# One transform of length 136 for whole graphs in place of two of length 80, in a two-layer graph network

## The chip, the cores and the metric

The kernel runs on one core of one Trainium2 chip. A core has five engines with an instruction queue each: TensorE (PE: matrix multiplies; its weight loads are listed apart as PEld), VectorE (DVE), ScalarE (ACT), GpSimd (POOL) and SyncE (SP). In this kernel SP only issues DMAs, and ACT issues some beside its own work; all DMAs run on the same 16 DMA engines. The metric is the device time of one execution in microseconds (us). Everything is float32. In the profile one float32 multiply is two MATMUL records, so counts of records are twice those of the matmul calls in the code.

## The reference, cut to what matters

128 graphs of 128 nodes with 256 features go through two layers, each with a layer norm, a relu and a residual around it. The change concerns the convolution path of layer 0:

```python
h = relu(layernorm(x))                      # 128 graphs x 128 nodes x 256
h1 = relu(bn1(conv1(h)))                    # conv1: width 1, 256 -> 256
h2 = bn2(conv2(h1))                         # conv2: 17 taps along the nodes, padding 8, 256 -> 256
x_conv = relu(h2 + h)
A = exp(-dist(h @ w_se.T)) * adj            # the edges
x_nmp = A @ relu(h @ w_msg.T)               # the messages
out = GRU([x_conv, x_nmp], h)               # the gates r, z, n
```

conv2 is computed through a Fourier transform along the nodes: transform the taps once, transform the graphs, multiply each frequency by a 256x256 matrix, transform back.

## The kernel before, in words

Blocks of four graphs (`BB`), 32 of them. conv2 takes windows of 64 outputs (`OUTW`) with a transform of length `LW` = 80, so a graph is two windows; 80 rows of a transform are 40 pairs (`NP_`), real and imaginary part. The program runs in five stages.

1. **Heads, first half** (blocks 0 to 15, function `heads`). Per block: layer norm (`head_stats`, `head_norm` on DVE, one POOL power), transpose to features on partitions and relu (`head_turn`, L212 and L213, which also stores the result to DRAM, `htd`), conv1 (`head_conv1`, L226 to L230), and the transform of its output (`head_spectra`, L241), whose results are copied from PSUM into `X`, a tile in SBUF with all frequencies of 64 graphs (`HG`), by DVE (L247) and ACT (L249). In between, `some_spectra` makes the taps' transforms (`weight_spectra`, L165): 8 units of 64 output channels (`WCH`), each 64 matmul calls on 17 of 128 partitions, four at once on four groups of 32 partitions, copied to `sp` (two buffers, L171 and L173) and stored by one DMA per unit to `vd` in DRAM (L175).
2. **Frequencies, first half** (`spectral`). For each pair, six matmul calls of 256 columns (three real products, L312 and L317; pair 0 has four calls, L302), with a sum of the weights on POOL (L309), a combination of `X` on DVE (L307), a copy on ACT (L314) and the final add on DVE (L318). The weights `v` come from `vd` by SP (L294, three buffers of two pairs), the results `ys` go to `yd` in DRAM four pairs at a time (L321).
3. **Heads, second half**, blocks 16 to 31, into the same `X`. The weights of the gates are loaded here.
4. **Frequencies, second half**, with sums of the gates' weights on POOL between the pairs (`gate_weights`).
5. **Gates.** Per block: messages (L516), the inverse transform (`conv_out`: for each half of the channels four calls of 128 columns on `ym`, L498, and one of 256 columns on `yr`, L501, into one PSUM bank; then one DVE and one ACT instruction, L504 and L505), edges (L536, L548, L551 to L553), the messages' sums (L563), the GRU's products (L612) and layer 1 (L877, L937 and others) turn by turn. `beside_gates` is a generator that says in which turn each part of the next block stands; what it doesn't use of the turns goes to layer 1. `load(i)` fetches a block's `ht`, `at`, `ym`, `yr` on SP.

In the first stage the order on all engines is the order written in the program. From then on POOL, and until the last stage of frequencies SP too, keep the written order; the others are placed by the scheduler of the language. PSUM has eight banks, taken in turn (`bank`).

Of the kernel before, what the change touches and what calls it, by code (L numbers as in the profile page):

```python
# [13 lines left out]
P = 128  # L14
EPS = 1e-5
KW = 17
PAD = 8
BB = 4
HG = 64
OUTW = 64  # L20
LW = 80
NP_ = LW // 2
WCH = 64
NR = 2 * LW - P
# [50 lines left out]
def gnn_kernel(ctx: ExitStack, tc: tile.TileContext, io, out0: bass.AP, out1: bass.AP):  # L75
# [6 lines left out]

    NBH = HG // BB
    NH = B // HG

    cst = ctx.enter_context(tc.tile_pool(name="cst", bufs=1))
    front = ExitStack()
    hc = front.enter_context(tc.tile_pool(name="hc", bufs=1))
# [13 lines left out]
    fd = hc.tile([P, 2 * LW], F32)  # L102
# [46 lines left out]
    vd = dram.tile([C, D // WCH, P, LW, WCH], F32, tag="vd", name="vd")  # L149
    yd = [dram.tile([HG, 2, LW, D], F32, tag=f"yd{h}", name=f"yd{h}") for h in range(NH)]  # L150

# [6 lines left out]
    def weight_spectra(pool, c, q, w2):  # L158

        sp = pool.tile([P, LW, WCH], F32, tag="sp", name="sp", bufs=2)  # L160
        for t in range(WCH // 16):
            ps = [bank() for _ in range(4)]
            for j in range(4):
                for r in range(4):
                    nc.tensor.matmul(ps[r][:, j * LW:(j + 1) * LW], w2[32 * r:32 * r + KW, 4 * t + j, :],  # L165
                                     gt[32 * r:32 * r + KW, :], start=True, stop=True)
            for r in range(4):
                o0 = t * 16 + 4 * r
                dst, s = sp[:, :, o0:o0 + 4], ps[r][:, :4 * LW].rearrange("p (j d) -> p d j", j=4)
                if r == 3 and t < WCH // 16 - 1:  # L170
                    nc.vector.tensor_copy(dst, s)  # L171
                else:
                    nc.scalar.copy(dst, s)  # L173
            yield
        nc.scalar.dma_start(vd[c, q], sp)  # L175
# [56 lines left out]

    def head_spectra(X, i):
        h1 = h1s.pop(i)
        g0 = (i * BB) % HG
        for c in range(C):
            xv = X[:, c].rearrange("p a k (w g) -> p (a k) w g", w=2)
            for h in range(BB // 2):
                ps = bank()
                for bb in range(2):  # L240
                    nc.tensor.matmul(ps[:, bb * 2 * LW:(bb + 1) * 2 * LW], h1[:, 2 * h + bb, c * P:(c + 1) * P], fd,  # L241
                                     start=True, stop=True)
                s = ps[:, :4 * LW].rearrange("p (g w d) -> p d w g", g=2, w=2)
                dst = xv[:, :, :, g0 + 2 * h:g0 + 2 * h + 2]
                for w in range(2):
                    if h:
                        nc.vector.tensor_copy(dst[:, :, w], s[:, :, w])  # L247
                    else:
                        nc.scalar.copy(dst[:, :, w], s[:, :, w])  # L249

    def heads_begin(wk, xk, ahead, h):

        i = h * NBH
        for k in range(ahead):
            head_load(xk, ahead, i + k, nc.scalar)
        yield
        for k in range(3):
            head_stats(wk, i + k)
            yield
            if k < 2:  # L260
                head_norm(i + k)
        head_turn(wk, i)

    def heads(wk, xk, ahead, X, h, between):

        i0, i1 = h * NBH, (h + 1) * NBH
        for i in range(i0, i1 + 1):
            if i + ahead < i1:
                head_load(xk, ahead, i + ahead, nc.sync)
            if i < i1:  # L270
                head_conv1(wk, i)
            between()
            if i + 1 < i1:
                head_turn(wk, i + 1)
            if i + 2 < i1:
                head_norm(i + 2)
            between()
            if i > i0:
                head_spectra(X, i - 1)
            if h == 0 and i % 2:  # L280
                between()
            if i + 3 < i1:
                head_stats(wk, i + 3, h1s[i] if h else None)

    def spectral(bp, X, h, amid):

        for p0 in range(0, NP_, 4):
            amid.get(p0, lambda: None)()
            ys = bp.tile([P, 4, 2, D], F32, tag="ys", name="ys", bufs=2)
            for p in range(p0, p0 + 4):  # L290
                if p % 2 == 0:
                    v = bp.tile([P, C, D // WCH, 4, WCH], F32, tag="v", name="v", bufs=3)
                    for c in range(C):
                        nc.sync.dma_start(v[:, c], vd[c, :, :, 2 * p:2 * p + 4, :].rearrange("q i d o -> i q d o"))  # L294
                vr, vi = v[:, :, :, 2 * (p % 2), :], v[:, :, :, 2 * (p % 2) + 1, :]
                a, d = X[:, :, p, 0, :], X[:, :, p, 1, :]
                y = ys[:, p - p0]
                ps = bank()
                if p == 0:
                    for k, (u, w) in enumerate(((a, vr), (d, vi))):  # L300
                        for c in range(C):
                            nc.tensor.matmul(ps[:, k * D:(k + 1) * D], u[:, c], w[:, c], start=c == 0, stop=c == C - 1)  # L302
                    nc.scalar.copy(y.rearrange("p k o -> p (k o)"), ps)
                    continue
# [3 lines left out]
                vs = bp.tile([P, C, D // WCH, WCH], F32, tag="vs", name="vs", bufs=3)  # L308
# [11 lines left out]
            for w in range(2):  # L320
                nc.scalar.dma_start(yd[h][:, w, 2 * p0:2 * p0 + 8, :].rearrange("g d o -> g (d o)"),  # L321
                                    ys[w * HG:(w + 1) * HG].rearrange("p a k o -> p (a k o)"))

# [7 lines left out]
    def gate_weights():  # L331
        tt = nc.gpsimd.tensor_tensor
        for k in range(3):
# [9 lines left out]
    with front as es:  # L343
        hk = es.enter_context(tc.tile_pool(name="hk", bufs=1))
        xp = es.enter_context(tc.tile_pool(name="xp", bufs=1))
        X = xp.tile([P, C, NP_, 2, P], F32)
        order = es.enter_context(ExitStack())
        order.enter_context(tc.manual_schedule(engines={nc.gpsimd.engine}))
        sync_order = order.enter_context(ExitStack())
        sync_order.enter_context(tc.manual_schedule(engines={nc.sync.engine}))  # L350
        with ExitStack() as ws:

            ws.enter_context(tc.manual_schedule())

# [5 lines left out]
            taps = [taps_load(wp, *todo[0], nc.sync, split=4)]  # L360
# [3 lines left out]
            def some_spectra(k=1):  # L364
                for _ in range(k):
                    if not spectra and todo:
                        spectra.append(weight_spectra(wp, *todo.pop(0), taps.pop(0)))
                    if spectra and next(spectra[0], STOP) is STOP:
                        spectra.pop(0)
                        if len(todo) > 1:  # L370
                            taps.append(taps_load(wp, *todo[1], nc.scalar))
                        some_spectra()
# [16 lines left out]
            some_spectra()  # L389
            next(consts)  # L390
            head_norm(1)
            head_stats(hk, 2)
            some_spectra()
            heads(hk, xk, ahead, X, 0, some_spectra)
# [3 lines left out]
        xk = es.enter_context(tc.tile_pool(name="xk1", bufs=1, reuse_waits="tile"))  # L398
        bp = es.enter_context(tc.tile_pool(name="bp", bufs=1, reuse_waits="tile"))
# [5 lines left out]
        sw = [gw.tile([P, 3, 3, P], F32, name=f"sw{k}") for k in range(3)]  # L405
# [6 lines left out]
        begin = heads_begin(hk, xk, 3, 1)  # L412
        sums = gate_weights()
        amid = {p: lambda: next(begin, None) for p in range(16, NP_, 4) if p != 20}
        spectral(bp, X, 0, amid)
        for _ in begin:
            pass

        def gate_loads():
            yield  # L420
            small_loads()
            yield
            yield
            nc.sync.dma_start(wih[:, :C], io["wih"][:D].rearrange("(c p) o -> p c o", p=P))
            yield
            yield
            nc.sync.dma_start(wih[:, C:], io["wih"][D:].rearrange("(c p) o -> p c o", p=P))
            yield
            yield
            nc.sync.dma_start(whh, io["whh"].rearrange("(c p) o -> p c o", p=P))  # L430

        loads = gate_loads()
        heads(hk, xk, 3, X, 1, lambda: next(loads, None))
        sync_order.close()
        spectral(bp, X, 1, {p: lambda: next(sums, None) for p in range(4, NP_, 4)})
# [3 lines left out]

    wk = ctx.enter_context(tc.tile_pool(name="wk", bufs=1, reuse_waits="tile"))  # L440
# [5 lines left out]
    def load(i):  # L446
        h, g0 = divmod(i * BB, HG)
# [6 lines left out]
        y = yd[h].rearrange("g w d o -> g (w d) o")[g0:g0 + BB]  # L454
        nc.sync.dma_start(ym, y[:, :P, :].rearrange("g r o -> r g o"))
        for b in range(BB):
            nc.sync.dma_start(yr[b * NR:(b + 1) * NR, :], y[b, P:, :])
# [3 lines left out]
    idr = wk.tile([P, BB, N - OUTW], F32)  # L461
# [28 lines left out]
    def conv_out(i):  # L490
# [3 lines left out]
        xc = wk.tile([P, C, T], F32, tag="xc", name="xc", bufs=2)  # L494
        for o in range(C):
            ps = bank()
# [671 lines left out]
```

## Time and profile before

Three runs took 1923.13, 1923.68 and 1927.98 us. The profiled execution took 1919.48 us, its span from the first to the last instruction 1917.7 us.

| stage | us from the span's start | length | PE busy | DVE | ACT | POOL | DMA share | GB/s |
|---|---|---|---|---|---|---|---|---|
| heads, blocks 0 to 15, and the taps | 0 to 173 | 173.0 | 160.3 | 113.2 | 87.7 | 22.0 | 0.81 | 298 |
| frequencies, first 64 graphs | 173 to 280 | 107.0 | 106.0 | 55.8 | 16.3 | 49.6 | 0.84 | 276 |
| heads, blocks 16 to 31 | 280 to 386 | 106.0 | 104.2 | 79.0 | 48.9 | 18.9 | 0.52 | 190 |
| frequencies, last 64 graphs | 386 to 489.5 | 103.5 | 102.7 | 49.1 | 15.0 | 57.7 | 0.83 | 279 |
| gates and layer 1 | 489.5 to 1917.7 | 1428.2 | 1417.1 | 1006.8 | 552.5 | 460.9 | 0.36 and 0.34 | 95 |

A busy PE in the profile is one with a matmul in flight, not one at its peak: matmuls overlap in the pipeline, so what an instruction costs is read from the distance between the starts of two groups, not from the mean time of one. The DMA share is the part of the time for which the 16 engines carried packets; packets that overlap can push it over 1.

### The profile page before, as it was taken

What the parts mean: (1) busy time and instruction counts of PE and PEld (TensorE: products, weight loads), DVE (VectorE), ACT (ScalarE), POOL (GpSimd) and SP (SyncE); (2) the same over time, 40 slices, a digit from 0 to 9 for tenths busy, and PEclk for the clock granted to TensorE, in tenths of its full rate; (3) what the DMA queues carried; (4) which work ended last, traced back from release to release, by engine and by line L of the source; (5) the groups of instructions that cost most, each with busy time, mean ns of one, the idle gap of its engine ahead of it and who ended that gap; (6) DMA issues with size and microseconds to landing.
All of it is one profiled execution on the core that took longest, in us unless ns stands there. A gap on an engine that the chain in (4) does not pass through costs nothing.

```text
span 1917.7 us, 30432 instructions
## 1 busy us (share of the span) xinstructions
PE 1890.3 (99%) x10610; PEld 1646.4 (86%) x10610; DVE 1303.9 (68%) x3247; ACT 720.5 (38%) x1555; POOL 609.1 (32%) x678
## 2 busy tenths in 40 slices
PE   8999999999999999999999999999999999999998
PEld 7888889988788888888888888888888888888887
DVE  5676557744677777777666677777756677787643
ACT  4553114411333343343343443333343434334334
POOL 1012531255234334433322233433322233443300
PEclk9999999999999999999999999999999999999999
DMA  8786896379842333333234433233334434222135
GB/s 322 288 312 226 297 311 235 121 241 306 256 117 73 74 95 76 81 90 106 71 94 97 130 97 87 73 82 108 75 90 97 144 72 107 65 78 71 36 92 151
DMA packets 248872, 265.81 MB, mean 139 GB/s; under 512 B 106866, under 2 KB 223943, under 8 KB 244239
## 3 DMA queue, kind: packets, MB, share of 16 engines
q1 hardware_dynamic: 236639, 196.70, 36.9%
q10 hardware_dynamic: 12080, 67.16, 9.0%
q8 instruction: 85, 1.39, 0.3%
q14 instruction: 68, 0.56, 0.1%
HBM read 178.66 MB, written 85.14 MB: 138 GB/s over the span
## 4 chain that ended last, share of the span: by engine, by line
PE 88%; DMA 4%; DVE 4%; issue 2%; ACT 1%; POOL 1%; SPq 0%; ACTq 0%; POOLq 0%; DVEq 0%
PE bank L612 45%; PE bank L317 6%; PE bank L516 5%; PE bank L937 5%; PE bank L877 5%; PE bank L226 4%; PE bank L312 3%; PE bank L563 3%; PE bank L498 3%; PE bank L241 3%; PE bank L165 2%; PE bank L501 1%; PE bank L788 1%; PE bank L856 1%; DMA v<-vd 1%
## 5 line engine op out<-in xcount | busy, mean ns | idle before, releaser
L612 PE MATMUL bank<-t,sw 128*128 128x256 f32 x1152 | 291.6, 380 | 0.7 <-DVE u L504 0.7
L625 POOL TENSOR_TENSOR u<-u,m 128x256 f32<-128x256 f32 x128 | 93.2, 728 | 612.7 <-ACT m L623 545.0
L612 PEld LDWEIGHTS bank<-t,sw 128*128 128x128 f32 x1152 | 215.8, 191 | 31.1 <-issue 2.3
L612 PE MATMUL bank<-t,wih 128*128 128x256 f32 x768 | 197.2, 379 | 0.0
L612 PEld LDWEIGHTS bank<-t,wih 128*128 128x128 f32 x768 | 143.4, 190 | 19.3 <-issue 0.5
L309 POOL TENSOR_TENSOR vs<-v 128x512 f32<-128x512 f32 x78 | 101.3, 1318 | 114.8 <-DMA v<-vd 49.4
L516 PE MATMUL bank<-wms,ht 128*128 128x259 f32 x512 | 124.1, 385 | 0.0
L226 PE MATMUL bank<-wc,ht 128*128 128x256 f32 x512 | 121.4, 391 | 1.6 <-ACT ht L213 1.6
L612 PE MATMUL bank<-xn,wih 128*128 128x256 f32 x384 | 114.9, 381 | 3.6 <-DVE xn L566 3.6
L612 PE MATMUL bank<-t,whh 128*128 128x256 f32 x384 | 115.0, 381 | 0.0
L612 PE MATMUL bank<-xc,wih 128*128 128x256 f32 x384 | 114.8, 381 | 0.0
L937 PE MATMUL bank<-w,hh 128*125 128x256 f32 (+9 forms) x480 | 113.5, 380 | 1.0 <-DVE hh L882 1.0
L226 PEld LDWEIGHTS bank<-wc,ht 128*128 128x128 f32 x512 | 98.0, 196 | 16.7 <-ACT ht L213 3.5
L516 PEld LDWEIGHTS bank<-wms,ht 128*128 128x128 f32 x512 | 98.3, 192 | 15.1
L612 PE MATMUL bank<-ht,whh 128*128 128x256 f32 x384 | 109.9, 380 | 0.0
L877 PE MATMUL bank<-ax,w 128*128 128x500 f32 (+8 forms) x416 | 107.0, 396 | 0.7 <-DMA w<-in_w_dram 0.7
L520 ACT ACTIVATE msg<-msg 128x512 f32<-128x512 f32 x64 | 40.3, 630 | 174.1 <-DVE msg L517 174.1
L630 DVE TENSOR_TENSOR u<-bank,u 128x256 f32<-128x256 f32 x128 | 53.7, 420 | 73.6 <-PE bank L612 73.5
L196 POOL TENSOR_TENSOR rs<-ve,mhalf 128x4 f32<-128x4 f32 x32 | 32.3, 1009 | 217.8 <-DVE ve L194 217.8
L307 DVE SCALAR_TENSOR_TENSOR s<-X 128x256 f32<-128x256 f32 x78 | 47.3, 612 | 79.4 <-PE bank L317 79.1
L937 PEld LDWEIGHTS bank<-w,hh 128*125 128x125 f32 (+9 forms) x480 | 84.3, 177 | 19.2 <-DVE hh L882 1.4
L657 ACT ACTIVATE nn<-nn,vec 128x512 f32<-128x512 f32 x64 | 46.2, 722 | 133.4 <-DVE nn L656 133.4
(187 smaller groups left out, 4279.5 us busy)
## 6 DMA issues: line engine op xcount, KB each, us to landing
v<-vd SPq DMA_DIRECT2D x80, 512.0 KB
vd<-sp ACTq DMA_DIRECT2D x8, 2560.0 KB
yd<-ys ACTq DMA_DIRECT2D x40, 512.0 KB
w<-in_w_dram SPq DMA_DIRECT2D x40, 512.0 KB
htd<-ht ACTq DMA_DIRECT2D x32, 512.0 KB
ht<-htd SPq DMA_DIRECT2D x32, 512.0 KB
ym<-yd SPq DMA_DIRECT2D x32, 512.0 KB
xt<-in_xT_dram SPq DMA_DIRECT2D x32, 512.0 KB
```

What stands on the lines that cost most here:

```text
L226: nc.tensor.matmul(pv[:, bb, :], ht[:, c, b * N:(b + 1) * N], wc1[:, c, :], start=c == 0, stop=c == C - 1)
L241: nc.tensor.matmul(ps[:, bb * 2 * LW:(bb + 1) * 2 * LW], h1[:, 2 * h + bb, c * P:(c + 1) * P], fd, start=True, stop=True)
L309: nc.gpsimd.tensor_tensor(vs, vr, vi, op=ALU.add)
L312: nc.tensor.matmul(p1[:, :D], a[:, c], vs[:, c], start=c == 0, stop=c == C - 1)
L317: nc.tensor.matmul(ps[:, k * D:(k + 1) * D], u[:, c], w[:, c], start=c == 0, stop=c == C - 1)
L498: nc.tensor.matmul(ps[:, b * N:(b + 1) * N], ym[:, b, o * P:(o + 1) * P], idm, start=b == 0, stop=False)
L516: nc.tensor.matmul(ps[:, :D + 3], ht[:, c, b * N:(b + 1) * N], wms[:, c, :], start=c == 0, stop=c == C - 1)
L563: nc.tensor.matmul(ps[:, b * N:(b + 1) * N], msg[:, b, c * P:(c + 1) * P], e[:, b, :], start=True, stop=True)
L612: nc.tensor.matmul(ps, w, d, start=n == 0, stop=n == len(pairs) - 1)
L625: nc.gpsimd.tensor_tensor(got["u4"], got["u2"], got["m5"], op=ALU.add)
L877: nc.tensor.matmul(pv[:, q - q0, :], w1s[k5 + g][:, c, q * P:(q + 1) * P], xv[:, c], start=c == 0, stop=c == C - 1)
L937: nc.tensor.matmul(ps[:n1, :D], hh[:, q, at:at + n1], w2s[k5 + g][:, q, :], start=q == 0, stop=q == HID // P - 1)
```

## The change

The transform has length 136, which holds a whole graph with its padding (128 + 16 would be 144; 136 is enough because what wraps around falls on the padding's zeros). `X` then holds 68 pairs for all 128 graphs, so there is one stage of heads for all 32 blocks and one of frequencies. `X` takes 139 KB of a partition, so the taps are transformed in 32 units of 16 output channels instead of 8 of 64, two half units per block of heads, over nearly the whole stage. `vd` has a new layout, [c, pairs of pairs, partition, unit, 4, 16]: a load of `v` reads 4 KB in one piece per partition (1 KB pieces before), and the store of a unit writes pieces of 256 bytes (20 KB before). `ys` is stored pair by pair, 2 KB pieces (8 KB before). In `conv_out`, 128 of the 136 rows are `ym` and the other 8 are `yr`, multiplied on four groups of 32 partitions; four PSUM banks are held at once, eight DVE instructions take the place of two, and all of it stands in one turn. `edges` stands four turns later relative to the messages. The sums of the gates' weights for one of the three matrices are made after the stage of frequencies, in a tile opened there; `X` is now the first tile on its side of the memory, with the tiles of the gates stage over it.

```diff
-HG = 64
-OUTW = 64
-LW = 80
+LW = 136
-WCH = 64
-NR = 2 * LW - P
+WCH = 16
+NR = LW - P
...
-    vd = dram.tile([C, D // WCH, P, LW, WCH], F32, tag="vd", name="vd")
-    yd = [dram.tile([HG, 2, LW, D], F32, tag=f"yd{h}", name=f"yd{h}") for h in range(NH)]
+    vd = dram.tile([C, NP_ // 2, P, D // WCH, 4, WCH], F32, tag="vd", name="vd")
+    yd = dram.tile([B, LW, D], F32, tag="yd", name="yd")
...
-        for t in range(WCH // 16):
+        n = WCH // 4
+        for j0 in range(0, n, 2):
+            jn = 2
             ps = [bank() for _ in range(4)]
-            for j in range(4):
+            for j in range(jn):
                 for r in range(4):
-                    nc.tensor.matmul(ps[r][:, j * LW:(j + 1) * LW], w2[32 * r:32 * r + KW, 4 * t + j, :],
+                    nc.tensor.matmul(ps[r][:, j * LW:(j + 1) * LW], w2[32 * r:32 * r + KW, j0 + j, :],
...
-        nc.scalar.dma_start(vd[c, q], sp)
+        nc.scalar.dma_start(vd[c, :, :, q].rearrange("u i d o -> i u (d o)"), sp.rearrange("p (u d) o -> p u (d o)", d=4))
...
                 for bb in range(2):
-                    nc.tensor.matmul(ps[:, bb * 2 * LW:(bb + 1) * 2 * LW], h1[:, 2 * h + bb, c * P:(c + 1) * P], fd,
+                    nc.tensor.matmul(ps[:, bb * LW:(bb + 1) * LW], h1[:, 2 * h + bb, c * P:(c + 1) * P], fd,
...
-                for w in range(2):
-                    if h:
-                        nc.vector.tensor_copy(dst[:, :, w], s[:, :, w])
-                    else:
-                        nc.scalar.copy(dst[:, :, w], s[:, :, w])
+                if h:
+                    nc.vector.tensor_copy(dst, src)
+                else:
+                    nc.scalar.copy(dst, src)
...
-                    v = bp.tile([P, C, D // WCH, 4, WCH], F32, tag="v", name="v", bufs=3)
-                    for c in range(C):
-                        nc.sync.dma_start(v[:, c], vd[c, :, :, 2 * p:2 * p + 4, :].rearrange("q i d o -> i q d o"))
+                v = bp.tile([P, C, D // WCH, 4, WCH], F32, tag="v", name="v", bufs=3)
+                for c in range(C):
+                    nc.sync.dma_start(v[:, c], vd[c, p // 2])
...
-            for w in range(2):
-                nc.scalar.dma_start(yd[h][:, w, 2 * p0:2 * p0 + 8, :].rearrange("g d o -> g (d o)"),
-                                    ys[w * HG:(w + 1) * HG].rearrange("p a k o -> p (a k o)"))
+            nc.scalar.dma_start(yd[:, 2 * p:2 * p + 2, :], y)
...
-        for o in range(C):
-            ps = bank()
+        pg = [bank()[:, :C * N].rearrange("p (o n) -> p o n", o=C) for _ in range(BB)]
+        for b in range(BB):
+            for o in range(C):
+                nc.tensor.matmul(pg[b][:, o, :], ym[:, b, o * P:(o + 1) * P], idm, start=o == 0, stop=False)
+
+        for o in range(C):
             for b in range(BB):
-                nc.tensor.matmul(ps[:, b * N:(b + 1) * N], ym[:, b, o * P:(o + 1) * P], idm,
-                                 start=b == 0, stop=False)
-
-            nc.tensor.matmul(ps.rearrange("p (b n) -> p b n", b=BB)[:, :, OUTW:], yr[:, o * P:(o + 1) * P], idr,
-                             start=False, stop=True)
-            u = wk.tile([P, T], F32, tag="el", name="u", bufs=2)
-            nc.vector.scalar_tensor_tensor(u, ps, sc2[:, o:o + 1], ht[:, o, :], op0=ALU.mult, op1=ALU.add)
-            nc.scalar.activation(xc[:, o, :], u, AF.Relu, bias=sh2[:, o:o + 1])
-            yield
+                g = slice(32 * b, 32 * b + NR)
+                nc.tensor.matmul(pg[b][:, o, :], yr[g, o * P:(o + 1) * P], idr[g, :], start=False, stop=o == C - 1)
+        for b in range(BB):
+            g = slice(b * N, (b + 1) * N)
+            for o in range(C):
+                nc.vector.scalar_tensor_tensor(xc[:, o, g], pg[b][:, o, :], sc2[:, o:o + 1], ht[:, o, g],
+                                               op0=ALU.mult, op1=ALU.add)
+        for o in range(C):
+            nc.scalar.activation(xc[:, o, :], xc[:, o, :], AF.Relu, bias=sh2[:, o:o + 1])
+        yield
...
             for _ in inverse:
                 yield
+            next(ends, None)
+            yield
+            yield
+            yield
+
             edges(i)
-            yield
-            next(ends, None)
             yield
             yield
             yield from x_nmp(i)
```

## The prediction

> **What bounds the kernel now.** I read the page first, for the busy share of the engines and the DMAs slice by slice, and then the stages (the table above).
>
> ```profile
> PE 1890.3 (99%) x10610; PEld 1646.4 (86%) x10610; DVE 1303.9 (68%) x3247; ACT 720.5 (38%) x1555; POOL 609.1 (32%) x678
> DMA  8786896379842333333234433233334434222135
> ```
>
> PE is the bound almost everywhere: 27 us of idle in the span, so time is won by fewer or narrower matmuls and lost where PE waits. The DMA row names the danger: in the first 13 slices, the stages that change, the DMAs are busy at 0.5 to 0.9. Next, PE's groups, for counts:
>
> ```profile
> L317 PE MATMUL bank<-v,s 128*128 128x256 f32 x312 | 80.6, 381 | 1.0 <-issue 0.8 <-DVE s L307 0.2
> L312 PE MATMUL bank<-vs,X 128*128 128x256 f32 x312 | 80.5, 379 | 0.8 <-POOL vs L309 0.8
> L241 PE MATMUL bank<-fd,h 128*128 128x160 f32 x512 | 78.1, 307 | 2.3 <-ACT X L249 2.3
> L165 PE MATMUL bank<-gt,w 17*128 17x80 f32 x1024 | 42.9, 301 | 7.7 <-DMA gt<-in_gt_dram 3.9 <-DMA w<-in_w2t_dram 2.4 <-DVE X L247 0.7
> ```
>
> Costs are read from starts in PE's timeline. A block of heads without taps:
>
> ```profile
> 305.37 3.62 PE L226 MATMUL bank<-wc,ht 128*128 128x256 f32 x16
> 308.82 1.04 PE L212 MATMUL bank<-ident,ln 128*128 128x128 f32 x8
> 309.69 2.34 PE L241 MATMUL bank<-fd,h 128*128 128x160 f32 x16
> 311.87 1.46 PE L226 MATMUL bank<-wc,ht 128*128 128x256 f32 x6
> ```
>
> It costs 3.45 + 0.87 + 2.18 = 6.50 us: 0.216 per record of 256 columns, 0.136 of 160, 0.109 of 128; 136 columns come to 0.116 on this line. With taps between:
>
> ```profile
> 114.77 3.62 PE L226 MATMUL bank<-wc,ht 128*128 128x256 f32 x16
> 118.32 1.13 PE L165 MATMUL bank<-gt,w 17*128 17x80 f32 x32
> 119.38 1.09 PE L212 MATMUL bank<-ident,ln 128*128 128x128 f32 x8
> 120.40 1.18 PE L165 MATMUL bank<-gt,w 17*128 17x80 f32 x32
> 121.52 2.44 PE L241 MATMUL bank<-fd,h 128*128 128x160 f32 x16
> ```
>
> From 114.77 to 121.52 is 6.75 us, less 3.45 and 0.87 leaves 1.215 us per group of 32 such records. A smaller group on four row groups is that of the edges:
>
> ```profile
> 1147.60 0.59 PE L612 MATMUL bank<-t,whh 128*128 128x256 f32 x2
> 1148.13 0.50 PE L548 MATMUL bank<-lt 5*128 5x128 f32 x8
> 1148.56 0.70 PE L612 MATMUL bank<-ht,sw 128*128 128x256 f32 x2
> 1149.10 0.59 PE L612 MATMUL bank<-t,sw 128*128 128x256 f32 x2
> ```
>
> 1.50 us for it and two pairs of 0.43: 0.63 us for 8 records. The line through 8 and 32 gives 0.83 us for 16, of which 0.43 doesn't depend on the number. Last, DMAs that write pieces of 412 bytes to DRAM (block outputs, 703 to 705 us):
>
> ```profile
> GB/s 338 321 338 321 321 321 330 272 280 247 214 231 140 115 99 132 124 99 131 99 82 90 178 96 161 112 72 120 128 112 104 128 176 96 144 88 24 80 16 136
> DMA packets 831, 0.33 MB, mean 165 GB/s; under 512 B 831, under 2 KB 831, under 8 KB 831
> ```
>
> They start at 330 GB/s (338/16 engines: 19.5 ns per piece) and fall to about 110 within 0.7 us of this window.
>
> **What the Trainium skill says.** *TensorEngine Tiling (Array Packing)*, Key Properties: a change of tiling mode drains TensorE; the 0.43 us per group agrees. *DMA: Bandwidth & Descriptors*, Why small descriptors are slow: a fixed 3 cycles per packet, 11 instead of 8 for 256 bytes; with its 435 GB/s over 16 engines that is an estimate of 13 ns per piece. The same page, Specifications: under 512 bytes the engine does a read-modify-write; the fall to 110 GB/s fits that, but those pieces also begin and end at odd addresses, and the new ones are aligned 256 bytes, which no row of before shows. Its section Issuing engines are not separate DMA queues: ACT's and SP's transfers share the 16 engines, so `vd` stores delay the loads of `x` too.
>
> **The change part by part**, in span time.
>
> *Frequencies.* Before: 952 records (L317 624, L312 312, L302 16) x 0.216 = 205.6 us, in 210.5. After: 67 pairs x 12 + 8 = 812, 175.4 us: 30.2 less. One start of a stage instead of two, and the 1 us of block 16's transposes is elsewhere: I allow 3 us of stalls instead of 4.9. 178.5, so -32. DMAs: per pair 0.79 MB in 2.6 us as before, loads in 4 KB pieces instead of 1 KB, stores in 2 KB. POOL's sum (1318 ns) reads runs of 16 elements instead of 64; up to 2.6 us per pair it stays hidden behind PE, and I take it unchanged, as its count of elements is. DVE (0.61 + 0.68 us) and ACT (0.37 and one DMA issue) have room too.
>
> *Heads, PE.* Per block 3.45 + 0.87 + 16 x 0.116 = 6.18 instead of 6.50; two half units of 0.83 each: 7.83 us. Together 32 x 6.18 + 64 x 0.83 = 251 us against 32 x 6.50 + 32 x 1.215 = 247. So on PE alone nothing is won. In the first stage of before 10.2 us passed per block (the chain has L241 at 102.0, 112.6, 121.6 and 132.7) with 6.5 + 2.5 x 1.215 = 9.5 of work: 0.7 of waiting.
>
> *Heads, the others per block.* ACT: 7 tap copies (355 ns for 320 elements, about 0.33 for 272), 2 of `ht` at 0.55, 2 of `h` at 0.63, 2 of `X` at 0.33, three DMA issues at 0.33 to 0.45: 6.5 us. DVE: 8 statistics (2.3), 4 norms (1.4), 2 adds (1.4), two copies of `X` and one of taps (1.2): 6.3. DMA: 1.31 MB of `x`, `ht` and taps at the 369 GB/s of the best window of the first stage, 3.55 us, and 4352 pieces of 256 bytes, 272 per engine. At 13 ns: 3.5; at 19.5, the flowing price of a larger piece: 5.3; I take 15: 4.1. Sum 7.65 us (7.1 to 8.85). Three resources thus stand at 6.5 to 7.8 us, and `sp` has two buffers: unit n+2 may be copied only when the store of unit n has landed, about one block after its issue. Behind that ACT copy stand the next `ht`, `h` and `X` copies, for which PE's banks wait. I take PE's 7.83 and the 0.7 of waiting: 8.5. The stage: 18 us until block 0 (20 before, a smaller first load of taps), 30 x 8.5, two blocks without taps at 6.4, the last transform 1.9: 288 us against 173 + 106 = 279. +9.
>
> *Heads to frequencies.* The tiles of the frequency stage lie over those of the heads: in the order of the built program the first load of `v` waits for one of the last L241. Two loads of 512 KB and their latency: PE idle 4.5 us. Before, they were issued from 148.6 us on, 24 us ahead of the stage. +4.5.
>
> *Frequencies to gates.* Before, `ht`, `at` and `ym` of block 0 were loaded while frequencies ran:
>
> ```profile
> 477.57 0.52 SPq L452 DMA_DIRECT2D ht<-htd  x1
> ...
> 494.85 0.34 SPq L452 DMA_DIRECT2D ht<-htd  x1
> ```
>
> with L317 until 489.5; only block 1's load waited for `X`. Now block 0's waits too, behind it all of SP's queue, and `ym` for the last `yd` store. PE is idle some 3.5 us; part of it is taken from the 3.6 us that L612 waits for `xn` at 505. +3.
>
> *Gates.* `conv_out`: 16 K=8 records in one row-tiled group 0.83 instead of 4 x 0.216 = 0.86: nothing. DVE: 8 x about 0.25 instead of 2 x 0.75, 0.5 us more per block, hidden as DVE is busy 77% there; uncovered it would be 16 us in all. The later edges keep a matmul order without a wait that the trace shows. The third weight sum, 4.3 us on POOL, precedes gates that need POOL only later. 0.
>
> Sum: -32 + 9 + 4.5 + 3 = -15.5. The profiled execution (1919.5) would become 1904; the median of the runs is 4.2 above it: **1908 us**.
>
> **Rivals.**
> *The stores make the DMAs the bound of the heads*, without a penalty for writes: at 19.5 ns or with ACT held at issuing (issues behind full queues took up to 2.0 us, 37 us into the span), a block takes 9.0 to 9.7 us, the stage 303 to 324: 1923 to 1944. For it: DMA share 0.81 already in the first stage. Against: the average needed, 78 MB in 288 us = 271 GB/s, is below the 298 there. It decides from 8.8 us per block, so against the likeliest case the sign turns at about 18.5 to 19.5 ns per piece.
> *Narrow writes back up* as the 412-byte ones did: 30 ns per piece (double) gives 8.2 + 3.55 = 11.7 us per block, +105 us, 2010; the 110 GB/s give 10.1 + 3.55, +165 us, 2075 or more. For it: the fence above. Against: alignment, and the stores of 4000-byte pieces, whose ends are odd too, run at 404 GB/s (1089.5 to 1090.5 us).
> *The heads stay at PE's 7.83*, for the two half units are evened out over the stage: 20 us better, 1888.
> *That the change does less than it says* can't be: the matmuls are counted in the program.
>
> **How the numbers follow.** Likeliest 0.47 (its own range 1895 to 1917), stage at PE 0.10, DMA-bound 0.24, narrow writes 0.19. About 0.3% is what a measurement of this kernel can tell: faster means under 1917.9, slower over 1929.5. Faster 0.56 (the first two, less 0.01), same 0.10 (0.09 of it from the DMA-bound case, whose low end is there), slower 0.34. The range runs from 1885 to 2015: it holds the first three cases and the mild half of the fourth.
>
> **What would show it.** L317 and L312 near 268 records each per line and product, frequencies in 176 to 181 us; a heads stage with blocks of 8.5 us and L241 groups of 1.86. DMA share in the heads under 0.9 says the stores flow; near 1, with ACT `sp` waiting for `vd<-sp` and PE for ACT, is the second case, and packets at under 200 GB/s the third. Wrong otherwise: POOL at more than 2.6 us per pair, or L612 waiting for DVE in the gates.

## The result, and the profile after

The changed kernel takes 2145.45 us (median of 4 runs, 2142.83 to 2148.35) against 1923.41 us before (4 runs): a ratio of 1.1163, 95% interval 1.1139 to 1.1187. The forecast was 1908 us with a range up to 2015; it missed on the slow side. The spans of the profiled executions are 2142.6 and 1917.7 us, 224.9 us apart, and that difference is accounted for below.

The page of the changed kernel, its engines and the rows of TensorE's granted clock and of the DMAs in 40 slices:

```profile
PE 1959.1 (91%) x10854; PEld 1682.7 (79%) x10854; DVE 1297.4 (61%) x3361; ACT 739.6 (35%) x1586; POOL 585.1 (27%) x667
PEclk8878877789999999999999999999999999999999
DMA  7555565559997423323243333423423342331225
```

TensorE idles 183 us instead of 27. In the first nine slices, the heads, its clock is at 0.7 to 0.8 and the DMAs are at 0.5 to 0.7: nothing is full there, and yet the stage is slow. The stages, read from TensorE's timeline as before:

| stage | before, us | after, us | difference | forecast |
|---|---|---|---|---|
| heads | 173.0 + 106.0 | 481.0 | +202.0 | +9 |
| idle between heads and frequencies | in the stages | 4.0 | +4.0 | +4.5 |
| frequencies | 107.0 + 103.5 | 180.2 | -30.3 | -32 |
| idle between frequencies and gates | in the stages | 4.7 | +4.7 | +3 |
| gates and layer 1 | 1428.2 | 1472.8 | +44.6 | 0 |

The groups of TensorE that answer to those shown of before (columns: records | busy us, mean ns | idle before them and what ended it):

```profile
L298 PE MATMUL bank<-v,s 128*128 128x256 f32 x268 | 68.8, 379 | 0.0
L293 PE MATMUL bank<-vs,X 128*128 128x256 f32 x268 | 69.9, 384 | 1.1 <-POOL vs L290 1.1
L241 PE MATMUL bank<-fd,h 128*128 128x136 f32 x512 | 114.4, 410 | 0.0
L165 PE MATMUL bank<-gt,w 17*128 17x136 f32 x1024 | 87.2, 366 | 122.2 <-ACT sp L173 118.1 <-DMA w<-in_w2t_dram 4.1
```

The frequencies have the 268 records a line and product that were forecast. In the heads the durations differ: L241 takes a mean of 410 ns for 136 columns, where 160 columns took 307 before, and L165 waits 118 us for ScalarE's copies of `sp`. What ScalarE does meanwhile is in its own timeline of one block, its transfer issues (ACTq) and the copies behind them, with idle time and what ended it in brackets:

```profile
207.23 0.38 ACTq L175 DMA_DIRECT2D vd<-sp  x1
207.65 4.89 ACTq L153 DMA_DIRECT2D w<-in_w2t_dram  x1
212.64 1.25 ACT L173 COPY sp<-bank 128x272 f32<-128x272 f32 x4 [4.78 <-issue]
...
214.91 0.33 ACTq L214 DMA_DIRECT2D htd<-ht  x1
...
222.29 0.38 ACTq L175 DMA_DIRECT2D vd<-sp  x1
222.71 4.14 ACTq L153 DMA_DIRECT2D w<-in_w2t_dram  x1
```

The store of 4352 pieces (L175) itself is issued in 0.38 us. The next issue on ScalarE, the taps load of L153, takes 4.89 us, and the copies stand behind it. From one block's first L226 to the next it is now 14.9 us in the median (14.0 to 17.1) instead of the 8.5 forecast. TensorE in the same block:

```profile
208.09 0.50 PE L165 MATMUL bank<-gt,w 17*128 17x136 f32 x4
213.07 1.56 PE L165 MATMUL bank<-gt,w 17*128 17x136 f32 x12 [4.49 <-ACT sp L173]
214.56 3.50 PE L241 MATMUL bank<-fd,h 128*128 128x136 f32 x16
217.90 3.62 PE L226 MATMUL bank<-wc,ht 128*128 128x256 f32 x16
```

After the wait, L241's 16 records take 3.34 us from start to start; the forecast had 1.86. The windows of two microseconds over it (columns: busy us of PE, PEld, DVE, ACT and POOL, then the granted clock, the DMA share and GB/s) say why:

```profile
207.00:209.00 2.00, 1.59 (x19) 1.15 (x12) 1.48 (x5) 0.63 (x1) 0.00 (x0) 1.00 0.40 89
209.00:211.00 2.00, 0.00 (x0) 0.00 (x0) 0.00 (x0) 0.00 (x0) 0.00 (x0) 0.90 0.99 221
211.00:213.00 2.00, 0.00 (x0) 0.00 (x0) 0.00 (x0) 0.36 (x2) 0.00 (x0) 0.50 0.86 186
213.00:215.00 2.00, 1.93 (x14) 1.68 (x15) 0.27 (x1) 1.88 (x6) 0.00 (x0) 0.50 1.17 354
215.00:217.00 2.00, 2.00 (x11) 2.00 (x11) 0.39 (x2) 1.26 (x4) 0.00 (x0) 0.50 0.92 368
217.00:219.00 2.00, 2.00 (x13) 1.87 (x13) 1.08 (x4) 0.39 (x1) 0.00 (x0) 0.89 0.01 2
```

The clock falls to 0.50 during the wait and stays there for some 4 us of the work behind it. All compute engines stand still from 209 to 211 us, while the DMAs run, and at 217 to 219 the DMAs stand still: store and work overlap only in part.

In the gates the loss has one name. TensorE's waits from 670 us on (us in total, times, longest), and the place in one block:

```profile
PE bank L753 <- ACT hn L749: 36.0, 28, 2.3
PE bank L481 <- DMA ht<-htd: 4.7, 1, 4.7
PE bank L577 <- DVE xc L467: 3.2, 1, 3.2
```

```profile
1307.69 0.38 PE L740 MATMUL bank<-ident,xl 128*100 128x128 f32 x2
1307.91 1.03 PE L577 MATMUL bank<-ht,whh 128*128 128x256 f32 x4
1310.17 0.98 PE L753 MATMUL bank<-ae,hn 100*128 100x212 f32 x4 [1.23 <-ACT hn L749]
```

Between the transposes of L740 and the matmul of L753, which needs their normalised result, lies one turn of gate matmuls. The kernel before has no wait at this matmul, its L788:

```profile
L788 PE MATMUL bank<-ae,hn 100*128 100x212 f32 x128 | 29.0, 349 | 0.0
```

There it was three turns: the second `yield` of `conv_out` and the turn of the edges lay between the two. In the changed kernel `conv_out` has only one `yield`, and `next(ends)` stands ahead of the edges and of the turns put before them.

### The profile page after: what moved, and what is told of

Its sections match the earlier page's. It is cut to its first block, busy times and chain, and to the rows that moved or that the text cites. A ratio compares the mean times of both kernels' runs of the same rounds, so it can differ in the third digit from the quotient of the medians.

```text
span 2142.6 us, 31052 instructions
## 1 busy us (share of the span) xinstructions
PE 1959.1 (91%) x10854; PEld 1682.7 (79%) x10854; DVE 1297.4 (61%) x3361; ACT 739.6 (35%) x1586; POOL 585.1 (27%) x667
## 4 chain that ended last, share of the span: by engine, by line
PE 82%; ACTq 6%; DVE 5%; DMA 3%; ACT 2%; POOL 1%; issue 1%; SPq 0%; DVEq 0%; POOLq 0%
PE bank L577 39%; ACTq L153 6%; PE bank L226 6%; PE bank L241 5%; PE bank L298 5%; PE bank L481 5%; PE bank L902 4%; PE bank L842 4%; PE bank L293 3%; PE bank L528 3%; PE bank L458 2%; PE bank L165 2%; PE bank L753 1%; DMA nt<-in_adjN_dram 1%; PE bank L821 1%; PE bank L463 1%
## 5 line engine op out<-in xcount | busy, mean ns | idle before, releaser
L165 PE MATMUL bank<-gt,w 17*128 17x136 f32 x1024 | 87.2, 366 | 122.2 <-ACT sp L173 118.1
L165 PEld LDWEIGHTS bank<-gt,w 17*128 17x128 f32 x1024 | 64.5, 227 | 143.8 <-ACT sp L173 124.3
L226 PE MATMUL bank<-wc,ht 128*128 128x256 f32 x512 | 128.0, 407 | 0.8 <-DVE wc L138 0.8
L173 ACT COPY sp<-bank 128x272 f32<-128x272 f32 x224 | 71.0, 400 | 146.8 <-issue 123.0
L226 PEld LDWEIGHTS bank<-wc,ht 128*128 128x128 f32 x512 | 105.2, 211 | 16.2 <-DVE wc L138 1.1
L290 POOL TENSOR_TENSOR vs<-v 128x512 f32<-128x512 f32 x67 | 86.7, 1311 | 101.8 <-DMA v<-vd 78.0
L241 PE MATMUL bank<-fd,h 128*128 128x136 f32 x512 | 114.4, 410 | 0.0
L171 DVE COPY sp<-bank 128x272 f32<-128x272 f32 x32 | 14.1, 441 | 164.7 <-ACT ht L213 158.4
L241 PEld LDWEIGHTS bank<-fd,h 128*128 128x128 f32 x512 | 107.0, 307 | 7.2 <-ACT ht L213 5.8
```

The source lines that it names most:

```text
L226: nc.tensor.matmul(pv[:, bb, :], ht[:, c, b * N:(b + 1) * N], wc1[:, c, :], start=c == 0, stop=c == C - 1)
L241: nc.tensor.matmul(ps[:, bb * LW:(bb + 1) * LW], h1[:, 2 * h + bb, c * P:(c + 1) * P], fd, start=True, stop=True)
L290: nc.gpsimd.tensor_tensor(vs, vr, vi, op=ALU.add)
```

## The experiments

**The store on the other queue.** Only the engine that issues the store is changed.

```diff
-        nc.scalar.dma_start(vd[c, :, :, q].rearrange("u i d o -> i u (d o)"), sp.rearrange("p (u d) o -> p u (d o)", d=4))
+        nc.sync.dma_start(vd[c, :, :, q].rearrange("u i d o -> i u (d o)"), sp.rearrange("p (u d) o -> p u (d o)", d=4))
```

> The store of the taps' spectra into vd is issued by SyncE in place of ScalarE; nothing else moves. Theory A (held issue: ScalarE stands at its next transfer issue, the taps load of L153, while the 4352 pieces of the store before it go out, 4.1 to 4.9 us a block): ScalarE's hold is gone, a block takes 8.5 to 9.3 us instead of 14.4 to 14.9, the heads end at 285 to 305 us instead of 480.9, TensorE's 123 us of waits for ScalarE's sp copies fall below 15, and the whole run takes 1950 to 1975 us; SyncE is held instead, at the x load behind the store, which five blocks of lead cover. Theory B (the pieces of 256 bytes cost the DMA engines the time, whoever issues them): blocks stay above 13 us and the run above 2100. Theory C (TensorE's clock of 0.81 over the heads makes them long by itself): the waits go but the clock stays, the heads take at least the 353 us that TensorE is busy in them now, and the run 2010 to 2020.

Measured: 1943.0 us, ratio to before 1.0135 (1.0112 to 1.0158), 202 us less than the changed kernel and just under the range of theory A. The heads end at 284.4 us and TensorE waits for no `sp` copy. The issue of L153 on ScalarE is back at 0.33 us in the median, and SyncE's next issue behind the store, a load of `x`, takes 1.71 instead of 0.37: the hold has gone over to SyncE, where nothing waits for it. The windows of the heads and of the frequencies in this kernel, then a block of its TensorE:

```profile
0.00:284.50 284.50, 270.92 (x2312) 233.24 (x2312) 196.79 (x593) 161.84 (x419) 34.75 (x41) 1.00 1.02 276
288.40:468.00 179.60, 178.94 (x812) 155.43 (x812) 93.84 (x132) 25.55 (x68) 94.71 (x78) 0.98 0.90 308
```

```profile
159.06 0.75 PE L165 MATMUL bank<-gt,w 17*128 17x136 f32 x16
159.73 1.09 PE L212 MATMUL bank<-ident,ln 128*128 128x128 f32 x8
160.75 1.11 PE L165 MATMUL bank<-gt,w 17*128 17x136 f32 x16
161.80 2.12 PE L241 MATMUL bank<-fd,h 128*128 128x136 f32 x16
163.75 3.62 PE L226 MATMUL bank<-wc,ht 128*128 128x256 f32 x16
167.30 0.75 PE L165 MATMUL bank<-gt,w 17*128 17x136 f32 x16
```

A block is 8.24 us, bound by TensorE, with the same pieces moved at 276 instead of 163 GB/s: theory B, that the pieces cost the DMA engines this time, falls. Theory C in its plain form falls as well, for the clock is 1.00 once the waits are gone. The section Issuing engines are not separate DMA queues of *DMA: Bandwidth & Descriptors* in the Trainium skill says that a second issuing engine only saves the sequencer's time to initiate a transfer, "which is usually small relative to the DMA itself". The second half doesn't hold here: an issue of 4.15 us in the median stood in a block of 14.9, the pieces of the store before it go out over 6.9 us in the trace, and moving that store won 202 us.

**The taps on the other queue.** The store stays on ScalarE.

```diff
-                        taps.append(taps_load(wp, *todo[1], nc.scalar))
+                        taps.append(taps_load(wp, *todo[1], nc.sync))
```

> The taps loads go to SyncE; the store into vd stays on ScalarE, whose next issue is then the ht store of L214, some 2.8 us later. Theory A (held issue, some 5.3 us from the start of the store): the hold moves to L214 and shrinks to 2 to 3 us a block, the heads end between 330 and 420 us, the run takes 1990 to 2085 us. Theory B (the DMA engines): no change, above 2100. If it were the taps load itself that is slow to issue, and not what stands before it on the queue: L214 at its 0.33 us and the run at 1950 to 1975.

Measured: 1968.36 us, ratio 1.0269 (1.0234 to 1.0303), below the range expected; the heads end at 306.5 us. ScalarE's timeline of a block:

```profile
156.24 0.37 ACTq L175 DMA_DIRECT2D vd<-sp  x1
...
158.24 1.13 ACT L213 ACTIVATE ht<-bank 128x512 f32<-128x512 f32 x2
159.41 1.88 ACTq L214 DMA_DIRECT2D htd<-ht  x1
```

The issue of `ht`, 0.33 us in the changed kernel, now takes 1.88: the hold has moved to whatever ScalarE issues next and ends 5.05 us after the start of the store (5.31 in the changed kernel). So it isn't the taps load that is slow. That the run is yet only 25 us slower than with the store on SyncE, where the range expected lay 47 to 142 us above that run, fits two readings of the trace: ScalarE does 2.8 us of useful copies before it stands, and the hold of 1.9 us that is left mostly falls into its slack, for TensorE waits for `sp` only 9.5 us in the whole stage and keeps its clock (0.99).

**Fewer pieces, and no pieces.** Both versions have the store on ScalarE and, besides, L753 two turns later (that edit by itself follows below, at 2099.2 us). The first lays `vd` out by rows, so that the store is one run per partition and the 256-byte pieces are met by the `v` loads. The second puts eight rows into a piece, half as many pieces of 512 bytes.

```diff
-    vd = dram.tile([C, NP_ // 2, P, D // WCH, 4, WCH], F32, tag="vd", name="vd")
+    vd = dram.tile([C, D // WCH, P, LW, WCH], F32, tag="vd", name="vd")
...
+        nc.scalar.dma_start(vd[c, q], sp)
...
+                    nc.sync.dma_start(v[:, c], vd[c, :, :, 2 * p:2 * p + 4, :].rearrange("q i d o -> i q d o"))
```

> On the version with L753 two turns later (2099.2 us): vd is laid out by rows of the spectra, so the same bytes leave on ScalarE as one long run of 8704 bytes for each partition, and the pieces of 256 bytes are met by SyncE's v loads in the frequencies instead (2048 pieces a load, 68 loads). Theory A by pieces (ScalarE is held by the number of pieces in the store before): L153 takes its 0.33 us, blocks 8.2 to 9 us, heads 280 to 300, as with the store on SyncE. Theory A by bytes (the same 1.1 MB in front of the taps hold the issue as long): heads stay above 450. The frequencies: 180 us if the v loads of 256-byte pieces keep up, for which 139264 pieces at 18.8 ns over 16 engines make 164 us; else up to 215. Whole run 1900 to 1940 by pieces, above 2090 by bytes.

```diff
-    vd = dram.tile([C, NP_ // 2, P, D // WCH, 4, WCH], F32, tag="vd", name="vd")
+    vd = dram.tile([C, NP_ // 4, P, D // WCH, 8, WCH], F32, tag="vd", name="vd")
...
+                v = [bp.tile([P, D // WCH, 8, WCH], F32, tag="v", name="v", bufs=3) for c in range(C)]
```

> On the version with L753 two turns later: vd keeps its order but with eight rows in a piece in place of four, so each store is 2176 pieces of 512 bytes, issued by ScalarE; v is held by channel half with three buffers in all, which makes the frequencies wait for loads (their time says nothing here). Read the heads only. Theory A by pieces: the hold at L153 falls from 4.2 us to about half, 1.8 to 2.6 us, and since 1.9 us of it stood hidden at L214 when the taps were on SyncE, blocks take 8.3 to 10 us. By bytes: the hold stays at 4 us and blocks above 13.

Measured: 1960.72 us for the rows, ratio 1.0223 (1.0187 to 1.0258); 2152.36 us for the halved pieces, of which some 60 us are waits for `v` in the frequencies, as announced. The rows miss their 1900 to 1940 in both stages: some issues of L153 still took up to 2.5 us and the heads end at 315, and the frequencies, whose loads now meet the 256-byte pieces, take 199 us instead of 180. The issue of L153 (ns, least, median and most), first with the pieces of 256 bytes (the run with L753 two turns later and nothing else changed), then in the two versions:

```profile
L153 ACTq DMA_DIRECT2D w<-in_w2t_dram x30: 3937/4162/6631, 13.7 to 449.1; - x30
```

```profile
L153 ACTq DMA_DIRECT2D w<-in_w2t_dram x30: 339/445/2507, 13.6 to 284.7; - x30
```

```profile
L153 ACTq DMA_DIRECT2D w<-in_w2t_dram x30: 1782/2063/4921, 13.6 to 404.1; - x30
```

With 4352, 2176 and 128 runs for the same bytes the median is 4.16, 2.06 and 0.45 us: the hold goes with the number of pieces in the store ahead, not with its bytes. (At equal bytes a smaller number means larger pieces; no run changes the one without the other.) ScalarE doesn't stand until the store is through, either: in the traces the pieces of 256 bytes go out over some 6.9 us and those of 512 over 4.6, both from about 1 us after the store's issue on, and ScalarE is free 5.3 and 2.4 us after it. Few pieces alone are no guarantee: the 2.5 us above stand behind 128 runs, as do the 2.00 us at 37.02 in the kernel before. This half of the expectation was right. The other half was wrong: with a hold of 2.06 us I had expected blocks of 8.3 to 10 us, and they took 13.5 in the median, the one shown next 13.1. TensorE's timeline shows where the rest went:

```profile
202.48 1.56 PE L165 MATMUL bank<-gt,w 17*128 17x136 f32 x12 [1.61 <-ACT sp L173]
203.97 4.00 PE L241 MATMUL bank<-fd,h 128*128 128x136 f32 x16
207.75 4.12 PE L226 MATMUL bank<-wc,ht 128*128 128x256 f32 x16
```

The wait is only 1.6 us, but L241 takes 3.78 us from start to start where the run with the store on SyncE has 1.95. Of the 13.1 us, 8.24 are the work at full clock and 1.6 the wait; 3.3 us more came in with the wait, and that needed a test of its own.

**Work in the place of the wait.** If the clock falls because TensorE waits, then useless matmuls put exactly there must shorten the run. The extra products, 15 in the version with pieces of 256 bytes and 6 in that with 512, go to an unused part of a bank; both have L753 two turns later.

```diff
                                     gt[32 * r:32 * r + KW, :], start=True, stop=True)
+                    if j0 and (j, r) == (0, 1):
+                        for _ in range(15):
+                            nc.tensor.matmul(ps[0][:, 2 * LW:3 * LW], ident, gt, start=True, stop=True)
```

> The changed kernel with L753 two turns later (2099.2 us), its store on ScalarE as it is, and 15 extra matmuls of 136 columns on all 128 rows (3.5 us at full clock, results overwritten) put at the point in each block where TensorE waits 3.7 to 4.5 us for ScalarE's sp copy. ScalarE's hold stays. Theory D (a wait of some us in each block is followed by half clock, which costs as much again as the wait): TensorE's clock in the heads rises from 0.81 to 0.95 or more, L241's 16 records take 1.9 to 2.1 us instead of 3.5 to 4.0, blocks 11.7 to 12.4 us instead of 14.6, the heads end at 395 to 415 us instead of 482, and the run takes 2010 to 2030 us although work was added. Rival (the lower clock comes from elsewhere, as from the transfers): clock unchanged, blocks as long or longer, the run 2095 to 2200.

> The same with the 512-byte pieces (2152.4 us; hold of 2.1 us and wait of 1.6 us a block, blocks of 13.1): six extra matmuls (1.4 us) at the wait. Theory D: clock in the heads from 0.78 to 0.95 or more, blocks 9.3 to 10 us, heads end at 315 to 335 us instead of 431, the run about 2045 to 2060. Rival: clock unchanged, blocks of 13 us or more, the run above 2145.

Measured: 2042.52 us, 57 less than without them, and 2092.1 us, 60 less than without. The mean clock over the heads goes from 0.81 to 0.98 in the first (windows 0 to 482 and 0 to 425.6 us), from 0.79 to 0.98 in the second (0 to 435.2 and 0 to 365.8). TensorE in the first of the two:

```profile
214.59 3.74 PE L169 MATMUL bank<-gt,ident 128*128 128x136 f32 x30
218.35 1.01 PE L165 MATMUL bank<-gt,w 17*128 17x136 f32 x12
219.29 2.12 PE L244 MATMUL bank<-fd,h 128*128 128x136 f32 x16
221.25 3.62 PE L229 MATMUL bank<-wc,ht 128*128 128x256 f32 x16
```

L169 is the filling, L244 and L229 the old L241 and L226, three lines further down. The hold of ScalarE is unchanged at a median of 4.19 us, 960 records of work were added, and a block falls from 14.8 to 12.4 us in the median because the work behind the wait runs at full clock; with the pieces of 512 bytes it falls from 13.5 to 11.0, where 9.3 to 10 had been expected. The heads end at 425.6 and 365.8 us, later than the 395 to 415 and 315 to 335 expected: in some blocks TensorE still waits, up to 2.1 us, and in the first version it then loses its clock again. The Trainium skill, *TensorE: Matmul & The Clock Gate*, Part 1: The HAM clock gate, has half rate after an idle window of about 3.4 us and full rate after about as long of sustained work. Half rate and its return to full agree: by the windows above (0.90 from 209 to 211 us, 0.89 from 217 to 219) the clock fell at 210.6 and rose at 217.4, after 4.4 us of work. The idle time doesn't, as counted here: the clock fell 2.0 us after TensorE had stopped, and waits of 1.4 to 1.6 us were enough with the pieces of 512 bytes. Whether the light records just before (17 rows in L165) count as idle wasn't tried. A short wait isn't enough by itself: the 28 waits at L753 in the gates, 1.3 us in the mean and up to 2.3, stand between full matmuls, and from 702 to 2090 us of that stage the clock is 1.00.

**The adjacency matmul two turns later**, with the heads as in the changed kernel.

```diff
             for _ in inverse:
                 yield
+            yield
+            yield
             next(ends, None)
-            yield
-            yield
             yield
 
```

> The changed kernel with the call that issues the adjacency matmul (L753) two turns later, so that three turns lie between the transposes of L740 and L753 as in the kernel before; the heads are untouched. Theory A (the one turn is too short for bn_stats, power, subtraction and the scaling on ScalarE that lie between the two): TensorE's 36 us of waits for hn at L753 fall below 4, and the run is 30 to 38 us shorter than the changed kernel, 2107 to 2117. Rival (VectorE's eight small operations of L467 hold its queue for 2.15 us, and TensorE waits for whatever of VectorE comes next): the wait moves to the next matmul behind VectorE's work, and less than 12 us are won.

Measured: 2099.2 us, ratio 1.095 (1.0925 to 1.0976), 46 us less than the changed kernel. The wait at L753 is gone:

```profile
L753 PE MATMUL bank<-ae,hn 100*128 100x212 f32 x128 | 28.3, 342 | 0.0
```

The wait didn't move elsewhere, so the rival falls. The gain is 8 to 16 us above what I expected; TensorE is busy 11 us less in the stage (1415.8 against 1426.7), which I have not traced further.

**The same distance in the kernel before.** Its `next(ends)` is put one turn behind the transposes, with its two large VectorE operations in `conv_out`.

```diff
+            next(ends, None)
             for _ in inverse:
                 yield
             edges(i)
             yield
-            next(ends, None)
             yield
```

> The kernel before with only the call that issues its adjacency matmul (L788) two turns earlier, one turn behind the transposes of L775, as in the changed kernel; its conv_out keeps two VectorE operations of 0.75 us. If the distance of one turn is the cause by itself: 28 to 30 waits for hn of about 1.2 us, 30 to 38 us more, a ratio of 1.015 to 1.020. If the eight small operations of the changed conv_out are needed to make VectorE late: under 10 us more, a ratio below 1.006.

Measured: 1961.73 us, ratio 1.0217 (1.0189 to 1.0245), somewhat above the expectation. TensorE's wait in it:

```profile
L788 PE MATMUL bank<-ae,hn 100*128 100x212 f32 x128 | 31.7, 371 | 36.4 <-ACT hn L784 36.4
```

The distance alone does it; the eight small operations aren't needed.

**Both mended, and a step further.** The store on SyncE and L753 two turns later:

> Both edits: the store issued by SyncE and L753 two turns later. Theory A for both: the gains add, 1915 to 1940 us, frequencies as in the changed kernel (180 us), heads 285 to 305, gates about 1440. If the heads keep a lower clock: up to 1985. Against the kernel before, with heads of 279, frequencies of 210 and gates of 1428: within 1% either way.

Measured: 1902.85 us (6 runs), ratio to before 0.9924 (0.9904 to 0.9944). Then the first `v` tiles are taken off the place where `fd` lies:

```diff
+    wp = hs.enter_context(tc.tile_pool(name="wp", bufs=1))
     hc = hs.enter_context(tc.tile_pool(name="hc", bufs=1))
...
-            wp = ws.enter_context(tc.tile_pool(name="wp", bufs=1))
```

> Store on SyncE and L753 two turns later (1902.9 us), and the pool with sp and w2 lies below that with gt, fd and wc1, so that the first v tiles lie over sp and w2, which come free with the last vd store, and no longer over fd, which the last L241 reads. If the first v load waits for that matmul, as the prediction said: TensorE's 3.9 us of idle between heads and frequencies fall below 1, the run takes 1898.5 to 1900.5 us. If it waits for the last vd store itself: no change, 1902 to 1904.

Measured: 1897.34 us (6 runs), ratio 0.9901 (0.9878 to 0.9924). TensorE at the border of the two stages:

```profile
279.72 3.87 PE L242 MATMUL bank<-fd,h 128*128 128x136 f32 x32
283.42 2.28 PE L284 MATMUL bank<-v,X 128*128 128x256 f32 x8
```

L242 and L284 are the old L241 and L283. The 3.9 us between them are gone, so that load waited for a tile's place, not for its data. With these three edits the single transform of length 136 is 1% faster than the kernel before.

## Why the prediction was wrong

**Frequencies: right.** 812 records, 180.2 us against 178.5, 30 us won against 32.

**Heads, PE: right at full clock.** With the hold away a block is 8.24 us, where the sum had 7.83 and, with waiting, 8.5; the stage is 284.4 us, where the forecast had 288.

**Heads, the others per block: this step failed.** It counted ScalarE's work as 6.5 us with "three DMA issues at 0.33 to 0.45". The price of an issue was read from rows in which no store of thousands of pieces stood ahead on the same queue. Behind one of 4352 pieces the issue takes 4.15 us in the median (3.9 to 6.7), in which ScalarE empties no bank; TensorE's waits for it come to 118 us in the stage, some 3.9 a block. The first rival named this very mechanism, "ACT held at issuing", but priced it at what the trace of before shows, 2.0 us, and bounded the block at 9.7. Those 2.0 us stood behind a store of 128 large pieces and could not say what 4352 cost; the issue is the term that was mis-sized, at 0.33 to 0.45 us in the sum and 2.0 in the rival, where 4.15 were measured.

**The clock: a term that was missing.** All costs of TensorE were taken at full clock, as the trace of before has it. From the changed kernel to the one with the store on SyncE, TensorE's busy time in the heads falls from 353.3 to 270.9 us and its idle time from 127.6 to 13.6: of the 196 us between them, 114 are waits and 82 the slower clock behind the waits.

**Narrow writes back up: no.** The 256-byte pieces took 18.8 ns in the mean in the heads of the changed kernel's trace, above the 15 that I took and inside the bounds, and the heads with the store on SyncE move 276 GB/s. The fall to 110 GB/s, for which the read-modify-write was cited, did not come; whether the 18.8 ns hold one, no run separates. Two totals of this rival don't follow from its blocks: 11.7 and 13.65 us a block make the heads 384 and 442 us long and the run 2004 and 2062, where it has 2010 and 2075. The sum of the first rival is no bound either: at the 18.2 ns a piece in the run with the store on SyncE it gives 8.5 us of DMA time a block, and the blocks took 8.24, with TensorE busy throughout and a DMA share of 1.02.

**Heads to frequencies, frequencies to gates: right.** 4.0 us and 4.7 us, for 4.5 and 3; that the first comes from the tiles' place is shown by the run that moved them.

**Gates: the second step that failed.** "The later edges keep a matmul order without a wait that the trace shows" looked at the edges and not at what was moved past them. `next(ends)` issues the adjacency matmul, and its distance to the transposes fell from three turns to one. (`edges` itself stands two turns later relative to the messages, not four as the description of the change has it: five turns lay before it and seven do now.) From the start of L740 it is 1.25 us of TensorE's work, and the chain of statistics, power, subtraction and scaling takes 1.23 us longer: 36 us of waits, and 46 us in the run. `conv_out` itself was priced well: TensorE loses nothing to its small products (L463's 16 records take 0.66 us), and VectorE's eight operations cost no wait beyond a single one of 3.2 us.

With the two failed steps undone the profiled execution takes 1907.0 us, where the sum had 1904: the heads are 3 us shorter than forecast and the gates 3 us longer, so the closeness is in part luck. The rest of the working held within such amounts; the two steps cost 237 us of the profiled execution.

## What to carry to other kernels

The number of pieces in a store is a cost of the engine that issues the next transfer on that queue, here about 1 us per thousand from 2176 to 4352 pieces, so a many-piece store belongs on an engine that has no copies to make. When a program's turns are counted out, every call that is moved must be followed to its producer and its consumer, and the distance measured in time on both sides. Where a change can make TensorE wait in every block, the work behind the wait may run at half clock and cost as much again: it did so behind waits of 1.4 to 4.5 us in the heads here, but hardly behind those of 1.3 us between the full matmuls of the gates.

## What the runs showed of the hardware that was not expected

- An issue behind a store of 4352, 2176 and 128 runs with the same bytes took 4.16, 2.06 and 0.45 us in the median.
- A wait of TensorE of 1.6 us in a block was followed by work at half clock, which cost more (3.3 us) than the wait; added matmuls in its place made the run 60 us shorter.
- Aligned stores of 256-byte pieces ran beside loads at 276 GB/s in all with no fall over time, where the ragged 412-byte ones of before fell to 110.
